# Order of the products in the first MLP unit: the product without inner weights is put first and held until its group is done

## The chip, the cores and the metric

The kernel runs on one core of a Trainium2 chip. The metric is the device time of that core in microseconds (us), from a run of the whole program. The engines are named as in the profile: PE is TensorE's matmul, PEld its weight load, DVE is VectorE, ACT is ScalarE, POOL is GpSimd, SP is SyncE (here an issuer of DMAs only).

## The reference, cut to what matters

There are two layers on x of shape (2, 512, 32, 32). Layer 0 is a deformable attention with a position bias from a small network, followed by an MLP; layer 1 is a single-head self-attention over 1024 positions. The change is in the MLP of layer 0:

```
x = x + out                                   # after the attention of layer 0
xn2 = _bn(x, bn2_g, bn2_b)
h1 = gelu(einsum('bchw,oc->bohw', xn2, mlp_w1) + mlp_b1)      # 512 -> 2048 channels
return x + einsum('bchw,oc->bohw', h1, mlp_w2) + mlp_b2       # 2048 -> 512
```

## The kernel before, in words

The MLP is cut into eight units: `units` holds (b, p) for two images b and four slices p of 512 hidden channels (L970). The loop over the units (L1185) loads the weights of later units, calls `layer1` for the slice's first matrix product with its gelu, and `layer2` for the second. Both are 512x512 by 512x1024 products in float32, done by Strassen's scheme in the form with seven block products: `PARTS` (L112) gives for product 1 to 7 the weight block and the data block, each an input quarter or a sum of quarters (`fold`, `spread`).

`layer1` applies the scheme twice. Six of the seven products (1 and 6, 4 and 7, 5 and 3, three groups) are themselves cut into seven small products by `twice` (L141). The weight blocks of these six need sums of their own quarters, the "inner weights" `we` (tile `w1e`): `load_inner` (L986) copies three quarters by DMA from SP and adds others on top by four accumulating DMAs from POOL (`gather`, L973), one after the other. The data blocks' inner sums are in `xe`, computed on DVE by `part` (L1082). The seventh product, number 2, is a plain one of 8 matmul instructions in the trace (L1073), with the weight quarter `w[:, 0]` and the data block `xb[:, 0]`, which are no sums. In the kernel before it is `second` (L1124): product into PSUM, added by DVE onto `c11`, then gelu of block 0.

The order is written out by hand. `STEPS` (L139) gives each of a group's seven small products a place in time: steps 1, 2, 6, 5, 7, 4, 3 at 0, 1, 3, 4, 6, 9, 12; group g is put 7g later, so that three groups interleave, and `fills` are put among them by the number that they carry: `second` at 21, and for the first unit of each image the parts 1 and 2 of the data sums at 4 and 10. Each entry's matmuls are chained behind the newest TensorE instruction, so TensorE keeps this order strictly. The other engines' order is chosen by the language's scheduler. In order of time (P2 is `second`):

```
place      0  1  2  3  4  5  6  7  8  9 10 11 12 13 14 15 16 17 18 19 20 21 22 23 24 25 26
group 0    1  2     6  5     7        4        3
group 1                         1  2     6  5     7        4        3
group 2                                              1  2     6  5     7        4        3
fill                                                                     P2
```

Within a group, steps 1, 6, 7 and 4 add up in one PSUM bank and are copied out by ACT in between (L166, L170, L172, L176), each before the next may add; steps 2, 5 and 3 are taken up by DVE (`plus`, L137). The last of them calls `done(g)` (L1110), which puts the groups' results together in `hm`:

- group 0 writes `c11` and `c12` (hm 0 and 1), group 1 `c21` and `c22` (hm 2 and 3), group 2 `r5` and `r3` (hm 4 and 5);
- `done(0)` adds c11 to c12; `done(1)` makes c22 and c21 and gives gelu of block 2; `done(2)` makes c22 and c12 and gives gelu of blocks 3 and 1.

`spread` then makes hm 4, 5, 3 and 6 out of the blocks, and `layer2` (L1133) multiplies them with `w2t` in the order of products 2, 1, 3, 5, 6, 7, 4, which read hm 2, 0, 3, 4, 5, 1, 6.

PSUM tiles of two banks come in turn from four buffers (`Turns`, L46 and L1184): `twice` takes two for each group, `second` one, `layer2` seven, 14 a unit. Before the first unit, TensorE does `project` (L1014), the output projection of the attention, whose last matmuls are at L1020.

Of the kernel before, what the change touches and what calls it, by code (L numbers as in the profile page):

```python
# [8 lines left out]
F32 = mybir.dt.float32  # L9
# [5 lines left out]
P = 128  # L15
# [42 lines left out]
def conv_seq_kernel(ctx: ExitStack, tc: tile.TileContext, x, xt, kst, pst, cst, vec, wsm, outw, w1, w2, wl, wlt, brow, out):  # L58
    nc = tc.nc
# [4 lines left out]
    def newest(engine):  # L64
        return next(i for i in reversed(nc.cur_bb.bb.instructions) if i.engine == engine)
# [8 lines left out]
    def col(name, i=0):  # L74
        return vs[:, VOFF[name] + i : VOFF[name] + i + 1]
# [60 lines left out]
    def plus(out, a, b_, op=ALU.add):  # L136
        nc.vector.tensor_tensor(out, a, b_, op)  # L137
# [3 lines left out]
    def twice(pool, sets, weights, moving, dest, done, fills=(), sign=-1.0):  # L141
        todo = [(7 * g + t, g, q) for g in range(len(sets)) for t, q in STEPS]
        todo += [(t, None, fill) for t, fill in fills]
        held = {}
        for _, g, q in sorted(todo, key=lambda e: e[0]):
            with tc.issue_after(newest(mybir.EngineType.PE)):
                if g is None:
                    q()
                    continue
                if q == 1:  # L150
                    held[g] = pool.tile([P, 2, 512], F32, tag="ps2", name="sw")
                if q == 2:
                    held[g, 2] = pool.tile([P, 2, 512], F32, tag="ps2", name="sw")
                bank = {2: lambda: held[g, 2][:, 0], 5: lambda: held[g, 2][:, 1], 3: lambda: held[g, 2][:, 1]}.get(
                    q, lambda: held[g][:, 0]
                )().rearrange("p (e n) -> p e n", e=2)
                s, t = PARTS[q]
                for e, p in enumerate(sets[g]):
                    for k, (w, x) in enumerate(zip(weights(p, s), moving(p, t))):
                        nc.tensor.matmul(  # L160
                            bank[:, e, :], w, x, start=(q in (1, 2, 5) and e == k == 0), stop=True,
                            skip_group_check=True,
                        )
            d11, d12, d21, d22 = (dest(g, m, h) for m in range(2) for h in range(2))
            if q == 1:
                nc.scalar.copy(d11, bank)  # L166
            elif q == 2:
                plus(d11, d11, bank)
            elif q == 6:
                nc.scalar.copy(d12, bank)  # L170
            elif q == 7:
                nc.scalar.activation(d22, bank, AF.Copy, scale=sign)  # L172
                b5 = held[g, 2][:, 1].rearrange("p (e n) -> p e n", e=2)
                plus(d22, d22, b5, ALU.subtract if sign < 0 else ALU.add)
            elif q == 4:
                nc.scalar.activation(d21, bank, AF.Copy, scale=sign)  # L176
            elif q == 3:
                plus(d12, d12, bank)
                done(g)
# [27 lines left out]
    with tc.tile_pool(name="lp", bufs=2) as lp:  # L207
# [381 lines left out]
        def weights(i):  # L589
            ps = [flat("psg") for _ in range(2)]  # L590
            for o in range(NCH):
                for k in range(NCH):
                    if i == 0 and (o, k) in ((1, 0), (3, 1)):
                        yield
                    nc.tensor.matmul(  # L595
                        ps[k // 2][:, k % 2 * 512 : k % 2 * 512 + 512], wls[i][:, 0, o, k * P : (k + 1) * P],
                        wls[i][:, 1, o, :], start=(o == 0), stop=(o == NCH - 1),
                    )
            yield
            for k2 in range(2):  # L600
                nc.scalar.copy(gs[:, i, 2 * k2 : 2 * k2 + 2, :].rearrange("p k o -> p (k o)"), ps[k2])
            yield
            nc.gpsimd.dma_start(out=gdr[i], in_=gs[:, i])
# [282 lines left out]
        for s in range(NS):  # L886
# [29 lines left out]
            if bg is None and s > ready and (s - ready) % 4 == 0 and (s - ready) // 4 <= 8:  # L916
                i = (s - ready) // 4 - 1
# [50 lines left out]
    with ExitStack() as top, tc.tile_pool(name="wp", bufs=1) as wp:  # L968
# [100 lines left out]
        def product(w, x):  # L1069
            def go(ps, a, b_):  # L1070
                for m in range(2):
                    for k in range(2):
                        nc.tensor.matmul(  # L1073
                            ps[:, m, :], w[:, a, k, m * P : (m + 1) * P], x[:, b_, k, :],
                            start=(k == 0), stop=(k == 1),
                        )
            return go
# [8 lines left out]
            part(0)  # L1086
            return xe, part

        def layer1(p, we, w, xb, xe, hm, others=()):
            def gelu(blk, src, scale=1.0):  # L1090
                for m in range(2):
                    nc.scalar.activation(
                        hm[:, blk, m, :], src[:, m, :], AF.Gelu,
                        bias=col("mb1", 4 * p + 2 * (blk // 2) + m), scale=scale,
                    )

            c11, c12, c21, c22, r5, r3 = (hm[:, j] for j in range(6))

            def weights(q, j):
                a = FIRST_W[PARTS[q][0]]  # L1100
                return [inner_w(w, we, a, a - 1)[j]]

            def moving(q, j):
                b_ = FIRST_X[PARTS[q][1]]
                return [inner_x(xb, xe, b_, b_ - 1)[j]]

            def dest(g, m, h):
                return hm[:, 2 * g : 2 * g + 2, m, 256 * h : 256 * h + 256]

            def done(g):  # L1110
                if g == 0:
                    plus(c12, c12, c11)
                elif g == 1:
                    plus(c22, c22, c12)
                    plus(c21, c21, c22)
                    gelu(2, c21, -1.0)
                else:
                    plus(c22, c22, r5)
                    gelu(3, c22, -1.0)
                    plus(c12, c12, r5)  # L1120
                    plus(c12, c12, r3)
                    gelu(1, c12)

            def second():  # L1124
                ps = mq.tile([P, 2, 512], F32, tag="ps2", name="sw")
                product(w, xb)(ps, 0, 0)
                plus(c11, c11, ps)
                gelu(0, c11)

            twice(mq, ((1, 6), (4, 7), (5, 3)), weights, moving, dest, done, ((21, second), *others))  # L1130
            spread([hm[:, j] for j in range(7)])

        def layer2(b, p, w, hm):  # L1133
# [41 lines left out]
        xb = normalise(0)  # L1175
        spread(op1[1])
        project(1, *op1, op1w[:, 3:5].rearrange("p a k n -> p a (k n)"))
        xe, part = sums(xb)
# [5 lines left out]
        mq = Turns([ctx.enter_context(tc.tile_pool(name="mq", bufs=1, space=PSUM)), zp, zp, zp])  # L1184
        for i, (b, p) in enumerate(units):  # L1185

            j, k = divmod(i, NCH)
            if k == 0:
                br = cp.tile([P, C], F32, tag="kz", name="br")
                nc.sync.dma_start(out=br, in_=brow[j].partition_broadcast(P))  # L1190
            wr = f_pool.tile([P, C], F32, tag="ss", name="wr")
            nc.sync.dma_start(out=wr, in_=wlt[:, i])
            with tc.issue_after(copied[-1]) if i else nullcontext():
                load_first(i + 1)
            wa, we, wb = wts.pop((b, p))
            hm = cp.tile([P, 7, 2, 512], F32, tag="big", name="hm")
            layer1(p, we, wa, xb, xe, hm, ((4, lambda: part(1)), (10, lambda: part(2))) if p == 0 else ())
            if i == NU:
                with tc.issue_after(newest(mybir.EngineType.DVE)):
                    finish(0)  # L1200
            load_inner(i + 1)

            with tc.issue_after(newest(mybir.EngineType.DVE)):
                nc.vector.scalar_tensor_tensor(
                    wr, wr, 1.0, br, ALU.mult, ALU.mult, accum_out=ub[:, j, k : k + 1]
                )
            if p == NU - 1 and b == 0:
                xb = normalise(1)
            layer2(b, p, wb, hm)
            load_second(i + 1)  # L1210
            if i == NU:
                with tc.issue_after(newest(mybir.EngineType.SP)):
                    gg = f_pool.tile([P, 7, 2, 256], F32, tag="vp", name="gg")
                    load_g(gg, 0)
            if i == NU + 2:
                xbl = blocks(0)
            if p == NU - 1 and b == 0:
                xe, part = sums(xb)
# [6 lines left out]
    with tc.tile_pool(name="sp", bufs=1) as sp:  # L1225
        for b in range(B):
# [180 lines left out]
            def moving(p, j):  # L1407
                g, e = where[p]
                x = ax(g, PARTS[p][1])[j] if j < 4 else (x45[g][:, 0], x45[g][:, 1], inner["x"][g])[j - 4][:, e]
                return [x[:, k] for k in range(2)]  # L1410
# [173 lines left out]
```

## Time and profile before

| | |
|---|---|
| median of 3 runs (lowest to highest) | 2621.48 us (2620.96 to 2621.51) |
| the profiled execution's own time | 2623.41 us |
| its span, first to last instruction | 2621.6 us |
| PE busy in the span | 2597.2 us, 99% |
| PEld, DVE, ACT, POOL busy | 1004.4, 2311.3, 1745.7, 981.8 us |
| mean granted TensorE clock | 0.999 |
| matmuls of `twice` in the first unit | from 1944.60 us of the span on |
| first matmul of `layer2` in the first unit | 1970.74 us |

The profile is one execution of the program. A busy PE is not PE at its peak, since matmuls are pipelined; so the idle time of PE and the granted clock in a stretch are read from the timeline and the windows rather than from the share. A row of a timeline has the start in us from the span's start, the length, the engine, the line in the kernel, the operation, what is written and read, shapes, the count of instructions merged into the row, and in brackets the idle time before it with what ended it. One logical float32 matmul appears as two matmul instructions.

### The profile page before, as it was taken

To read this page: it belongs to the slowest core of one execution; us is meant where nothing else is said; L and a number is where in the kernel's file an instruction comes from. 1 tells how busy PE (TensorE), PEld (TensorE's weight loads), DVE (VectorE), ACT (ScalarE), POOL (GpSimd) and SP (SyncE) were. 2 spreads that over 40 slices of the span, in tenths; PEclk is the share of its full clock that TensorE was granted. 3 is DMA by queue.
4 is the path that set the end of the run, shared out by engine and by line. 5 is a ranking of instruction groups with operands and counts; after the bars stand their busy time and mean duration, and the time that the engine had idled before them with its cause. 6 is when DMAs were issued, how large, how long until landed. Compare 5 with 4: busy or idle time off the path is not lost.

```text
span 2621.6 us, 48901 instructions
## 1 busy us (share of the span) xinstructions
PE 2597.2 (99%) x19648; PEld 1004.4 (38%) x19648; DVE 2311.3 (88%) x1462; ACT 1745.7 (67%) x2324; POOL 981.8 (37%) x1121
## 2 busy tenths in 40 slices
PE   9999999999999999999999999999999999999999
PEld 3332322233233233322233332332355665646556
DVE  7999999999999999999999999898776587666656
ACT  5887898888887888888887777777723242314041
POOL 1344544444445444444444454333332334200100
PEclk9999999999999999999999999999999999999999
DMA  5888988999999999899898999787777768400202
GB/s 190 174 191 186 213 183 184 195 200 201 189 191 194 188 204 195 180 190 201 186 202 181 196 193 193 163 181 166 160 198 162 153 139 177 90 16 0 73 0 57
DMA packets 177522, 428.27 MB, mean 163 GB/s; under 512 B 29936, under 2 KB 78208, under 8 KB 174608
## 3 DMA queue, kind: packets, MB, share of 16 engines
q0 software_dynamic: 107392, 273.09, 58.2%
q1 hardware_dynamic: 69472, 151.75, 17.4%
q8 instruction: 155, 2.54, 0.4%
q14 instruction: 71, 0.58, 0.1%
q10 hardware_dynamic: 432, 0.31, 0.0%
HBM read 82.16 MB, written 6.55 MB: 34 GB/s over the span
## 4 chain that ended last, share of the span: by engine, by line
PE 63%; DVE 12%; issue 10%; DMA 9%; POOL 4%; ACT 2%; DVEq 0%; SPq 0%; POOLq 0%; ACTq 0%
PE ps L693 37%; PE sw L1073 7%; PE sw L1234 7%; PE sw L160 6%; DVE h L676 5%; DMA u<-uc 3%; DVE ub L713 2%; POOL u L732 2%; PE sw L1332 2%; DMA u<-u 1%; PE psg L595 1%; DMA uc<-uc 1%; DVE hm L137 1%; DVE uo L713 1%; DMA w1e<-w1e 1%
## 5 line engine op out<-in xcount | busy, mean ns | idle before, releaser
L693 PE MATMUL ps<-h,cw 128*32 128x512 f32 x16384 | 1775.2, 593 | 10.8 <-ACT rx L703 7.7
L676 DVE CUSTOM_DVE_ANT_1 h<-ta,tb 128x4096 f32<-128x4096 f32 (+1 forms) x257 | 1130.1, 4398 | 20.8 <-PE ps L693 16.8
L693 PEld LDWEIGHTS ps<-h,cw 128*32 128x32 f32 x16384 | 525.7, 110 | 1229.3 <-issue 1132.9
L703 ACT ACTIVATE rx<-ps,sc 128x1024 f32<-128x1024 f32 x512 | 567.6, 1109 | 155.9 <-PE ps L693 97.5
L732 POOL DMA_DIRECT2D u<-u x397 | 410.1, 1516 | 14.6 <-DMA u<-ub 12.1
L705 ACT ACTIVATE ub<-ps,sc 128x1024 f32<-128x1024 f32 x256 | 307.8, 1202 | 84.0 <-PE ps L693 82.6
L713 DVE SCALAR_TENSOR_TENSOR ub<-rx,sc,ub 128x1024 f32<-128x1024 f32 x256 | 326.2, 1274 | 10.5 <-ACT ub L705 10.5
L715 POOL DMA_DIRECT2D uo<-ub x127 | 112.1, 883 | 584.2 <-DVE ub L713 536.7
L1073 PE MATMUL sw<-hm,w2t 128*128 128x512 f32 x448 | 193.9, 592 | 0.4 <-DVE hm L125 0.2
L705 ACT ACTIVATE uo<-ps,sc 128x1024 f32<-128x1024 f32 x128 | 153.9, 1202 | 42.4 <-PE ps L693 39.7
L713 DVE SCALAR_TENSOR_TENSOR uo<-rx,sc,uo 128x1024 f32<-128x1024 f32 x128 | 163.2, 1275 | 5.0 <-ACT uo L705 5.0
L732 POOL DMA_DIRECT2D u<-uc x126 | 126.8, 1269 | 19.4 <-DMA u<-uc 17.9
L715 POOL DMA_DIRECT2D uc<-ub x64 | 56.1, 877 | 199.7 <-DVE ub L713 158.9
L1073 PEld LDWEIGHTS sw<-hm,w2t 128*128 128x128 f32 x448 | 85.0, 190 | 104.8 <-issue 98.7
L137 DVE TENSOR_TENSOR hm<-hm,sw 128x512 f32<-128x512 f32 (+1 forms) x80 | 58.6, 737 | 74.4 <-PE sw L160 54.7
L715 POOL DMA_DIRECT2D u<-ub x64 | 55.4, 866 | 168.5 <-DVE ub L713 164.8
L732 POOL DMA_DIRECT2D uc<-uo x63 | 103.1, 1637 | 16.8 <-DMA uc<-uo 16.5
L732 POOL DMA_DIRECT2D uc<-uc x63 | 104.5, 1659 | 2.0 <-DMA uc<-ub 2.0
L1398 POOL DMA_DIRECT2D xs<-rs x6 | 7.2, 1200 | 258.1 <-DVE rs L137 258.1
L705 ACT ACTIVATE uc<-ps,sc 128x1024 f32<-128x1024 f32 x64 | 76.9, 1202 | 26.4 <-PE ps L693 16.6
L656 ACT ACTIVATE ta<-fb,vs 128x512 f32<-128x512 f32 (+1 forms) x65 | 89.2, 1376 | 6.5 <-DMA fb<-fdr 6.5
L732 POOL DMA_DIRECT2D u<-uo x63 | 83.3, 1322 | 24.7 <-DMA u<-uo 19.2
(294 smaller groups left out, 2624.9 us busy)
## 6 DMA issues: line engine op xcount, KB each, us to landing
uo<-ub POOLq DMA_DIRECT2D x127, 512.0 KB, 5.3
fb<-fdr SPq DMA_DIRECT2D x64, 512.0 KB, 6.1
u<-ub POOLq DMA_DIRECT2D x64, 512.0 KB, 6.7
uc<-ub POOLq DMA_DIRECT2D x64, 512.0 KB, 6.0
u<-u POOLq DMA_DIRECT2D x63, 256.0 KB, 7.0
u<-uo SPq DMA_DIRECT2D x63, 256.0 KB, 5.8
u<-uo POOLq DMA_DIRECT2D x63, 256.0 KB, 7.3
uc<-uc POOLq DMA_DIRECT2D x63, 256.0 KB, 8.0
```

Source lines behind the costliest of these rows:

```text
L137: nc.vector.tensor_tensor(out, a, b_, op)
L160: nc.tensor.matmul(bank[:, e, :], w, x, start=(q in (1, 2, 5) and e == k == 0), stop=True, skip_group_check=True,)
L656: nc.scalar.activation(ta.rearrange("p j x -> p x j")[:, :, j0:j1], fb[:, 0, :, j0:j1], AF.Identity, bias=col("cb1"), scale=col("w1x"),)
L676: nc.vector._custom_dve(TENSOR_ADD_SAT, out=h1[:, y : y + step].rearrange("p y t x -> p (y t x)"), in0=a.unsqueeze(1).to_broadcast([P, ste ...
L693: nc.tensor.matmul(ps[32 * q : 32 * q + 32, h, :], cw2[:, 32 * z : 32 * z + 32], h1[:, 16 * h : 16 * h + 16, q, :], start=True, stop=True,)
L703: nc.scalar.activation(o, ps, AF.Relu, bias=sc[:, 4 + z : 5 + z])
L705: nc.scalar.activation(o, ps, AF.Relu, bias=sc[:, 4 + z : 5 + z], scale=sc[:, z : z + 1])
L713: nc.vector.scalar_tensor_tensor(r[1], r[0], sc[:, z : z + 1], r[1], ALU.mult, ALU.add)
L715: nc.gpsimd.dma_start(out=sums[s][1], in_=sums[s][3], accum_op=ALU.add)
L732: nc.gpsimd.dma_start(out=out, in_=in_, accum_op=ALU.add)
L1073: nc.tensor.matmul(ps[:, m, :], w[:, a, k, m * P : (m + 1) * P], x[:, b_, k, :], start=(k == 0), stop=(k == 1),)
L1234: nc.tensor.matmul(ps[:, m, :], w[:, a, k, c + m * P : c + (m + 1) * P], x[b_][:, k, :], start=(k == 0), stop=(k == nk - 1),)
```

## The change

For the first unit alone (`i == 0`), product 2 is no longer done late, at 21, but before everything else, at -1. Its result can't be added to `c11` then, since group 0 has not written it. It is copied by ACT from PSUM to `r3` (hm 5), which group 2 will write later, and added to `c11` by DVE at 13.5: after `done(0)`, which must read c11 without it, and before the first step of group 2, whose copy overwrites part of `r3`. The gelu of block 0 follows there. In the other seven units nothing is changed.

```diff
-        def layer1(p, we, w, xb, xe, hm, others=()):
+        def layer1(p, we, w, xb, xe, hm, others=(), early=False):
...
-            twice(mq, ((1, 6), (4, 7), (5, 3)), weights, moving, dest, done, ((21, second), *others))
+            def first():
+                ps = mq.tile([P, 2, 512], F32, tag="ps2", name="sw")
+                product(w, xb)(ps, 0, 0)
+                nc.scalar.copy(r3, ps)
+
+            def merge():
+                plus(c11, c11, r3)
+                gelu(0, c11)
+
+            plain = ((-1, first), (13.5, merge)) if early else ((21, second),)
+            twice(mq, ((1, 6), (4, 7), (5, 3)), weights, moving, dest, done, (*plain, *others))
...
-            layer1(p, we, wa, xb, xe, hm, ((4, lambda: part(1)), (10, lambda: part(2))) if p == 0 else ())
+            layer1(p, we, wa, xb, xe, hm, ((4, lambda: part(1)), (10, lambda: part(2))) if p == 0 else (), i == 0)
```

## The prediction, made before the result was known

> **What bounds the kernel now.** I read the chain of work that ended last in order of time, then TensorE's own timeline around the start of the MLP, then the windows with the granted clock, then the timelines of VectorE and ScalarE. Columns of the chain and the timelines: start, length, what; in brackets the idle time before and its releaser.
>
> ```profile
> 1936.84 5.60 DMA w1e<-w1e
> 1942.72 13.25 DMA w1e<-w1e
> 1956.02 9.72 PE sw L160 x36
> 1965.74 3.43 PE sw L1073 x8
> 1970.90 24.03 PE sw L1073 x56
> ```
>
> The last sum of the inner weights of unit 0 is issued at 1942.72 and lands 13.25 us later. From 1956.02 on the chain is TensorE nearly without a break to the end of the kernel, so a microsecond saved or lost in unit 0 of the MLP is one of the total. TensorE in unit 0:
>
> ```profile
> 1944.60 1.89 PE L160 MATMUL sw<-xb,w1x 128*128 128x256 f32 x8
> ...
> 1956.02 1.13 PE L160 MATMUL sw<-xb,w1e 128*128 128x256 f32 x4 [2.19 <-DMA w1e<-w1e]
> 1956.98 4.44 PE L160 MATMUL sw<-xb,w1x 128*128 128x256 f32 x12
> 1961.26 1.03 PE L160 MATMUL sw<-xe,w1x 128*128 128x256 f32 x4
> ...
> 1963.85 1.03 PE L160 MATMUL sw<-xb,w1e 128*128 128x256 f32 x4
> ...
> 1965.58 3.60 PE L1073 MATMUL sw<-xb,w1x 128*128 128x512 f32 x8
> ...
> 1970.74 24.20 PE L1073 MATMUL sw<-hm,w2t 128*128 128x512 f32 x56
> ```
>
> Layer 1 lasts from 1944.60 to 1970.74, 26.14 us. Its work: one step of `twice` is 4 records in 0.86 us (1961.26 to 1962.12), 21 steps 18.1; the whole product at L1073 3.44 (1965.58 to 1969.01 for 8 records); together 21.56. So 4.58 us are lost: 2.19 in the wait for the weights, 1.69 in the 12 matmuls behind it (4.44 where the same group takes 2.75 elsewhere), 0.41 at the second pair of steps, 0.29 in crumbs. The 1.69 is the clock; its column is the one before the DMA share:
>
> ```profile
> 1957.00:1958.00 1.00, 1.00 (x5) 0.85 (x4) 0.71 (x2) 0.00 (x0) 0.63 (x1) 0.70 0.78 131
> 1958.00:1959.00 1.00, 1.00 (x4) 0.81 (x3) 1.00 (x1) 0.48 (x1) 0.00 (x0) 0.50 0.99 166
> 1960.00:1961.00 1.00, 1.00 (x4) 0.82 (x3) 0.00 (x0) 0.58 (x1) 0.33 (x1) 0.59 0.36 59
> ```
>
> Half speed from about 1957.4 to 1960.8, just after the gap. What VectorE and ScalarE do there decides the rest:
>
> ```profile
> 1957.19 0.69 DVE L137 TENSOR_TENSOR hm<-hm,sw 128x512 f32<-128x512 f32 x1 [5.15 <-PE sw L160]
> 1957.98 1.23 DVE L137 TENSOR_TENSOR hm<-hm 128x1024 f32<-128x1024 f32 x1
> 1959.15 0.69 DVE L137 TENSOR_TENSOR hm<-hm,sw 128x512 f32<-128x512 f32 x1
> ...
> 1965.78 0.60 ACT L172 ACTIVATE hm<-sw 128x512 f32<-128x512 f32 x1 [2.00 <-PE sw L160]
> 1966.39 1.28 ACT L1092 ACT_TABLE_LOAD   x1
> 1968.70 1.33 ACT L1092 ACTIVATE hm<-hm,vs 128x512 f32<-128x512 f32 x2 [1.02 <-DVE hm L137]
> ```
>
> The three VectorE rows are step 3 of group 0 taken up, done(0), and step 7 of group 1; on ScalarE the first gelu brings a table load, which runs when the instruction before it is over.
>
> **What the skill says.** The Trainium skill, "TensorE: Matmul & The Clock Gate", section "Part 1: The HAM clock gate", has two clock states, half after an idle window of about 3.4 us and full after a busy one. The trace agrees in the two states (1.00 and 0.50) and in the length of the low stretch (3.4 us), but here a gap of 2.19 us was enough. "ScalarE: Activation LUTs", section "What ACT_TABLE_LOAD costs", gives about 1.28 us for the load and as much again for a drain; the trace shows 1.28 and no drain beside it, so I use 1.28. "PSUM — Partial Sum Buffer", section "Engine vs sequencer instructions", calls the queues of ScalarE and VectorE strictly first in, first out; the timelines show no exception, and so a copy behind a gelu waits for the gelu.
>
> **The change part by part.**
>
> *The product moved to the front.* 8 matmul records, 3.44 us, at 1944.60: its weight quarter and its block of xb are there (w1x was loaded before its first sum at 1909.94, xb normalised by 1926.5), so nothing holds it. No DMA, SP or POOL instruction moves with it; the weights land at 1956.0 as before. Step 1 of group 0 starts at 1948.04. On ScalarE the new copy into r3 (128x1024, 1.01 us by the rows of L1138) ends about 1949.25, the copy of step 1 thus at 1949.8, and step 6 starts 0.15 late. VectorE's sums for xe now end before the take-up of step 2, so the 0.41 goes. Ten steps (8.63) then bring step 3 of group 0 to t = 1956.8. That is 0.8 after the landing: **the 2.19 goes, and its 1.69 with it**. If the landing came 0.8 later, part of it would be back.
>
> *The merge between the groups.* r3 lies where step 1 of group 2 is copied to (hm 4 and 5). So that copy waits for the merge on VectorE, and TensorE's step 6 of group 2, which adds on the same bank, waits for the copy. Without a wait it would come five steps after t, at t + 4.31. By the rows above: step 3 is taken up at t + 1.17, done(0) starts at t + 1.96, step 7 of group 1 at t + 3.13, the merge about t + 3.73, and ends at t + 4.96. Then ScalarE: the gelu pair of block 0 comes ahead of the copy in the program and is ready at the same moment, 1.33; the copy 0.58. The trace doesn't show this order. From both sides: copy first, TensorE goes on at t + 5.6 (stall 1.3); gelu first with its table load done while ScalarE was idle, t + 6.96 (2.65); gelu first with the copy of step 4 of group 1 (L176) ahead of both, t + 8.4 (4.1), for then the load starts only after L176: ready at t + 4.5, done t + 5.1, load to 6.4, gelu to 7.75, copy to 8.3. I take the last, because L176 is ready 0.45 before the merge ends and ScalarE is then idle. Behind the waiting step on TensorE is everything else. **+4.1.**
>
> *The clock after that gap.* 4.1 us is longer than the 2.19 that halved it before. The low stretch 1957.4 to 1960.8 gives windows that end at 1964.2 and 1967.6; the gap lies from 1961.1 to 1965.2, so half speed holds from 1964.2 to 1967.6, of which 2.4 us carry work. **+1.2** (between 0, no drop, and 1.7 as before).
>
> *The tail of layer 1.* The whole product stood between steps 7 and 4 of group 2 and covered two waits. Let s be the start of step 3 of group 1 (1963.85 before). The gelu of block 2 began at s + 4.85 (1968.70), its first half ends at s + 5.6, and layer 2's first product reads that. Before, layer 2 came at s + 6.89, so it was hidden by 1.3. Now four steps follow s, 3.45 us, and layer 2 can't start before s + 5.6: **+2.15**. The wait of step 4 for ScalarE's copy of step 7 (0.9) lies inside this. Later products of layer 2 need block 3 (about s + 8.2) and the spread (from s + 11.7) at s + 12.5 and later: no stall.
>
> *Downstream.* As many PSUM tiles per unit as before, the inner weights are freed at the same distance from layer 2: I cost it at nothing. The cover is the waiting time of the landed weights: unit 1's last sum is issued at 1990.84, and needed at 2003.66.
>
> *Sum.* Lost after: 0.15 + 4.1 + 1.2 + 2.15 = 7.6, before 4.58: **+3.0 us**. Layer 2 starts at about 1973.75 instead of 1970.74. The profiled execution took 2623.41 us (span 2621.6 and 1.8 around it) and would become 2626.4; the median of the runs is 2621.48 and becomes 2624.5, +0.11%. A measurement of this kernel tells some 0.2% from no change, 5.2 us; this is under it.
>
> **Rivals.**
> *A, table load hidden* (gelu ahead of L176): the stall is 2.65, and the clock drops for 1.7 or not at all: 0.15 + 2.65 + 1.7 + 2.15 = 6.65, +2.1, or +0.4. 2621.9 to 2623.6. For it: the load before ran without waiting. Against: L176 is ready earlier.
> *B, copy ahead of the gelu*: the stall is 1.3, too short for a clock drop: 0.15 + 1.3 + 2.15 = 3.6, -1.0. 2620.5. Against: later in program order.
> *C, the waits don't bind*: only 0.15 is lost, -4.4, 2617.1. It needs the copy of step 1 without the merge and block 2 a full 2 us earlier; the VectorE rows speak against both.
> *D, the clock makes it slower beyond doubt.* The profiled execution was 1.93 us longer than the median, about the clock's 1.69. If the timed runs don't have that drop, there is 1.69 less to win: +4.7, 2626.2; and if the tail's idle time of 2.15 halves the clock once more, +1.7: 2627.9, slower by 0.25%. It decides from gaps of about 2.2 us inside one window. Against: the runs agree within 0.6 us, so the drop comes in all or none, and the tail's gap is broken by two steps.
>
> **How the numbers follow.** Forecast 2624.5: 0.42. A 0.22, B 0.16, C 0.07, D 0.13. The range from 2620.3 to 2626.6 holds the forecast, A, B and the lower half of D, and leaves out C and the rest of D, some 0.14. Faster by over 0.2% (under 2616.2) asks for more than all that is lost: 0.02. Slower (over 2626.7) is the upper half of D: 0.07. Within: 0.91.
>
> **What would show it.** In the profile after: first product at about 1944.6; no wait for w1e at the third step of group 0; a gap of 4 us (A 2.65, B 1.3) before step 6 of group 2, released by ScalarE; the table load after L176; a low clock after it; layer 2 starting 5.6 us after step 3 of group 1, released by the gelu; its start at 1973.75. Wrong would be: the weights landing later than 1956.8, the gap absent, or new waits from unit 1 on.

## The result, and the profile after

| | before | after |
|---|---|---|
| median of 22 runs each (lowest to highest) | 2621.41 us (2620.12 to 2623.74) | 2625.38 us (2623.22 to 2626.82) |
| the profiled execution's own time | 2623.41 us | 2626.42 us |
| its span | 2621.6 us | 2624.7 us |
| first unit: first matmul of layer 1 to that of unit 1 | 1944.60 to 1994.77, 50.17 us | 1945.51 to 1998.26, 52.75 us |

The ratio of the times is 1.0015, with a 95% interval from 1.0009 to 1.0021: 4.0 us more, where 3.0 was predicted. The two spans differ by 3.1 us: 0.91 before the first unit begins, 2.58 in it, and -0.39 behind it. The change shows in the first unit alone.

TensorE's timeline after (columns as before):

```profile
1945.51 3.60 PE L1073 MATMUL sw<-xb,w1x 128*128 128x512 f32 x8
...
1957.84 1.03 PE L160 MATMUL sw<-xb,w1e 128*128 128x256 f32 x4
...
1961.30 1.03 PE L160 MATMUL sw<-xe,w1x 128*128 128x256 f32 x4
1966.12 3.78 PE L160 MATMUL sw<-xe,w1e 128*128 128x256 f32 x8 [3.80 <-ACT hm L166]
1969.70 1.91 PE L160 MATMUL sw<-xb,w1e 128*128 128x256 f32 x4
1971.40 1.11 PE L160 MATMUL sw<-xb,w1x 128*128 128x256 f32 x4
1972.39 1.13 PE L1073 MATMUL sw<-hm,w2t 128*128 128x512 f32 x2
1973.35 1.03 PE L160 MATMUL sw<-xe,w1x 128*128 128x256 f32 x4
```

The whole product comes first. The step that waited 2.19 us for the inner weights in the kernel before (here at 1957.84) waits for nothing. In its place step 6 of group 2, due at 1961.30 + 0.86 = 1962.16, starts at 1966.12, released by ScalarE's copy. The rows behind it are slow: 8 records in 3.58 us where they take 1.73 elsewhere. And the records at L1073 that read `hm` are layer 2: they stand among the last steps of layer 1.

The chain of waits (start, length, what) goes from TensorE to ScalarE and back (L176 a copy, the piece without a tile the table load, the pair the gelus of block 0, L166 the copy that TensorE waits for):

```profile
1962.36 0.60 ACT hm L176
...
1962.97 1.28 ACT L1092
...
1964.27 1.33 ACT hm L1092 x2
1965.60 0.48 ACT hm L166
...
1966.12 6.39 PE sw L160 x16
```

VectorE's timeline in the same stretch, done(0) and the merge:

```profile
1959.70 1.23 DVE L137 TENSOR_TENSOR hm<-hm 128x1024 f32<-128x1024 f32 x1
...
1961.44 1.22 DVE L137 TENSOR_TENSOR hm<-hm 128x1024 f32<-128x1024 f32 x1
```

The last VectorE row is the merge, over at 1962.66. From the due time to it 0.50; until L176 is over 0.30; the table load 1.29; the gelu pair 1.26; the copy 0.56 (its row in the timeline is 1965.51 to 1966.07); TensorE's start 0.05: 3.96 us. The windows (busy share and count of PE, PEld, DVE, ACT, POOL, then the granted clock, DMA share, GB/s):

```profile
1964.00:1965.00 1.00, 0.00 (x0) 0.00 (x0) 0.00 (x0) 0.99 (x3) 0.00 (x0) 0.87 0.76 131
...
1968.00:1969.00 1.00, 1.00 (x4) 0.82 (x3) 0.00 (x0) 0.59 (x1) 0.00 (x0) 0.50 0.00 0
...
1971.00:1972.00 1.00, 1.00 (x5) 0.86 (x4) 0.35 (x1) 0.00 (x0) 0.00 (x0) 0.72 0.00 0
```

A clock of 0.87 is half speed for the last 0.26 us of its slice, 0.72 half speed for the first 0.56: low from about 1964.74 to 1971.56, 6.8 us, twice the 3.4 of the kernel before. The 16 records of layer 1 between 1966.12 and 1972.39 took 6.27 us where four steps take 3.45, so the low clock costs about 2.8 us in this execution.

**The account.** The unit's work is 21.56 (layer 1) + 24.08 (layer 2, 56 records of 0.43) = 45.64 us. Lost before: 50.17 - 45.64 = 4.53. Lost after: 52.75 - 45.64 = 7.11, of which 3.96 gap, 2.8 clock, and 0.28 behind the first copy (60 records of `twice` in 13.22 us, 12.94 of them work). For the end of layer 1 next to nothing is left, about 0.1.

### The profile page after: what moved, and what is told of

It reads as the page before. It is cut to its first block, busy times and chain, and to the rows that moved or that the text cites. A ratio compares the mean times of both kernels' runs of the same rounds, so it can differ in the third digit from the quotient of the medians.

```text
span 2624.7 us, 48900 instructions
## 1 busy us (share of the span) xinstructions
PE 2597.7 (99%) x19648; PEld 1005.3 (38%) x19648; DVE 2308.9 (88%) x1462; ACT 1748.3 (67%) x2325; POOL 977.8 (37%) x1121
## 4 chain that ended last, share of the span: by engine, by line
PE 75%; DVE 10%; issue 7%; DMA 4%; POOL 2%; ACT 2%; DVEq 0%; ACTq 0%; POOLq 0%; SPq 0%
PE ps L693 47%; PE sw L1073 7%; PE sw L160 7%; PE sw L1244 7%; DVE h L676 4%; PE sw L1020 2%; PE sw L1342 2%; DVE ub L713 2%; DMA u<-uc 1%; POOL u L732 1%; PE psg L595 1%; DMA u<-u 1%; PE sim L823 1%; DVE uo L713 1%; DVE hm L137 1%
## 5 line engine op out<-in xcount | busy, mean ns | idle before, releaser
L1073 PE MATMUL sw<-hm,w2t 128*128 128x512 f32 x448 | 194.3, 593 | 0.2 <-DVE hm L125 0.2
L137 DVE TENSOR_TENSOR hm<-hm,sw 128x512 f32<-128x512 f32 x79 | 57.6, 732 | 79.0 <-PE sw L160 54.4
L1073 PEld LDWEIGHTS sw<-hm,w2t 128*128 128x128 f32 x448 | 84.9, 190 | 103.9 <-issue 97.3
(295 smaller groups left out, 2621.9 us busy)
```

What stands on the lines that cost most here:

```text
L1073: nc.tensor.matmul(ps[:, m, :], w[:, a, k, m * P : (m + 1) * P], x[:, b_, k, :], start=(k == 0), stop=(k == 1),)
```

## The experiments

**The theory**: the gap comes from holding product 2 in `r3`, which the copy of step 1 of group 2 overwrites, so that merge, table load and gelu pair all stand ahead of TensorE's step 6; the clock falls because of the gap. **Rivals:** the place of the product itself costs (it stands ahead of the steps, and no longer covers the end); or the low clock comes from the change of order, not from the gap. Beside these, one question of the baseline: is the low clock of the kernel before in its timed runs, or in its profiled execution alone? Below, "the unit" is the length of the first unit in the profiled execution, and an interval is 95%, of the ratio to the kernel before as it ran beside the experiment (medians 2621.33 beside 1 to 4, 2621.30 beside 5 to 8, 2622.11 beside 9 and 10).

**1. Held in a bank that nobody writes.** `hm[:, 6]` is free until the end of the unit, so the copy of group 2 has no merge to wait for.

```
-                nc.scalar.copy(r3, ps)
+                nc.scalar.copy(hm[:, 6], ps)
-                plus(c11, c11, r3)
+                plus(c11, c11, hm[:, 6])
```

> Product 2 is held in hm 6, which nothing writes before the spread, in place of r3; all else as in the change. Theory (the loss is the copy of group 2's step 1 queued behind merge, table load and gelu, and the low clock after that gap): no gap before step 6 of group 2, no low clock, first unit (first matmul of layer 1 to first matmul of unit 1) 46.2 to 47.8 us against 52.91 with the change and 50.17 before; time about 2617.5 to 2619. Rival (what costs is that product 2 no longer stands in the tail of layer 1, and the extra copy): 2624 or more.

Measured: 2620.47 us, ratio 0.9997 (0.9989 to 1.0005); the unit took 47.41 us, 5.34 less than with `r3` (the 52.91 of the expectation ran to the end of the unit's last matmul; to the first matmul of unit 1, as for all others, it is 52.75). The time is above the 2617.5 to 2619 expected, since that was reckoned from a baseline which experiment 5 corrects. TensorE:

```profile
1961.45 2.28 PE L160 MATMUL sw<-xe,w1e 128*128 128x256 f32 x8
...
1965.42 1.10 PE L1073 MATMUL sw<-hm,w2t 128*128 128x512 f32 x2 [0.83 <-ACT hm L170]
```

Step 6 of group 2 comes when it is due, the clock stays full, and what is left is 0.38 in the row of 2.28 (1.89 elsewhere) and 0.83 ahead of the first records of layer 2. 3.96 + 2.8 went, and some 1.4 came. The gap and the low clock belong to `r3`. The place of the product costs in this unit no more than it gains by covering the wait for the weights (47.41 us against 47.77 and 48.56 in experiments 5 and 6); in units without that wait it does cost, as experiment 10 shows.

**2. Held in `r3`, gelu left where it was.** The merge stays at 13.5, the gelu of block 0 goes back to 21, behind the copy.

```
-                gelu(0, c11)
-            plain = ((-1, first), (13.5, merge)) if early else ((21, second),)
+            plain = ((-1, first), (13.5, merge), (21, lambda: gelu(0, c11))) if early else ((21, second),)
```

> Product 2 still held in r3 and merged at 13.5, but the gelu of block 0 is placed at 21, so the copy needn't wait for table load and gelu. Theory: the gap shrinks from 4.0 to about 1.3 us (merge and copy alone), too short for a low clock; first unit about 47.5 us, time about 2619. Rival (the wait for the merge is what counts, gelu and table load are beside it): gap about 4, time about 2625.

Measured: 2620.61 us, ratio 0.9995 (0.9987 to 1.0003); the unit 47.48 us.

```profile
1962.84 1.99 PE L160 MATMUL sw<-xe,w1e 128*128 128x256 f32 x8 [1.16 <-ACT hm L166]
```

The wait for the merge alone leaves a gap of 1.33 against the due time 1961.51, and no low clock: the gap and the time of rival B (1.3, 2620.5). The time is above the 2619 expected, for the same reason as in 1. Of the 3.96 us some 2.6 are thus the load and the gelu pair ahead of the copy.

**3. The table loaded ahead of time.** A gelu of one element in `first`, written where nothing reads it, brings the load into idle time; the gelu pair stays ahead of the copy.

```
                 nc.scalar.copy(r3, ps)
+                nc.scalar.activation(uc[:, 0:1], xb[:, 0, 1, 511:512], AF.Gelu)
```

> The change plus a one-element gelu on ScalarE while it is idle before layer 1, so that the table load is done there. Theory: gap 2.7 us in place of 4.0, released by the same copy; the clock still drops, for one window or two; first unit 50.3 to 51.6 us, time 2622.5 to 2624. Rival (ScalarE is not the one waited for): no change, 2625.4.

Measured: 2622.89 us, ratio 1.0005 (0.9997 to 1.0013); the unit 50.37 us. Its TensorE row, then its window with the low clock:

```profile
1964.78 3.46 PE L160 MATMUL sw<-xe,w1e 128*128 128x256 f32 x8 [2.38 <-ACT hm L166]
```

```profile
1965.00:1966.00 1.00, 1.00 (x4) 0.80 (x4) 0.45 (x1) 0.00 (x0) 0.00 (x0) 0.57 1.11 193
```

The gap is 2.55, so the load was worth 1.4. The clock still falls, at about 1965 (0.57), for one stretch of 3.4 us and not two. This is rival A (2.65 and 1.7; 2623.6) in size.

**4. The gap filled.** Eight matmul records that nothing needs stand at 16.5, with their own PSUM tile; nothing else is changed.

```
+            def busy():
+                ps = mq.tile([P, 2, 512], F32, tag="ps2", name="sw")
+                product(w, xb)(ps, 0, 0)
+
-            plain = ((-1, first), (13.5, merge)) if early else ((21, second),)
+            plain = ((-1, first), (13.5, merge), (16.5, busy)) if early else ((21, second),)
```

> The change plus eight unneeded matmul records (3.4 us) put in the gap before step 6 of group 2; their result is not used. Theory: the useful work waits as long as before (4.0 us) but TensorE stays busy, the clock stays full, and 2.8 us are saved: first unit about 50.1 us, time about 2622.6. If the clock costs only the 1.2 us of the prediction: about 2624.2. If it costs nothing: 2625.4.

Measured: 2623.86 us, ratio 1.0009 (1.0001 to 1.0017); the unit 50.34 us.

```profile
1961.85 3.70 PE L1073 MATMUL sw<-xb,w1x 128*128 128x512 f32 x8 [0.69 <-ACT hm L176]
1965.39 1.89 PE L160 MATMUL sw<-xe,w1e 128*128 128x256 f32 x8
```

Step 6 now comes 4.39 us after it is due (1961.00), later than in the changed kernel, and yet the unit is 2.41 us shorter: the records behind it run at full clock (1.89, not 3.78). The low clock follows from TensorE's idle time, not from the order, and costs in the two profiles what the account says (2.41 + 0.43 more wait = 2.84). In the medians the difference is only 2625.38 - 2623.86 = 1.52, which makes 1.95 for the clock: less than the expected 2.8, and the first sign that not every timed run of the changed kernel has the 6.8 us.

**5. The kernel before once more**, with only a comment changed.

```
-# ---- launch: one core ----
+# ---- launch: one core, again ----
```

> The kernel before once more, for more executions and their clocks. If the low clock after the 2.19 us gap comes in every execution, the profiled one has the first unit at 50.2 us again and lies near the median. If it depends on how the gap falls, an execution without it has the first unit at about 48.5 us, and the median run is nearer to that; then the change costs about 1.7 us more in the median than in the two profiles.

Measured: 2621.49 us, ratio 1.0000 (0.9992 to 1.0008). But its profiled execution took 2621.22 us, not 2623.41, and the unit 47.77, not 50.17:

```profile
1956.38 1.13 PE L160 MATMUL sw<-xb,w1e 128*128 128x256 f32 x4 [1.47 <-DMA w1e<-w1e]
1957.34 2.75 PE L160 MATMUL sw<-xb,w1x 128*128 128x256 f32 x12
```

The work ahead ended 1.07 us later in this execution (the unit starts at 1945.67), the wait for the weights is 1.47 and not 2.19, and the 12 records behind it take 2.75 and not 4.44. One program, two profiled executions, 2.2 us apart.

The timed runs say which is the rule, by their mean granted clocks, which are on record to three places. A stretch of 3.4 us at half speed takes 1.7 us of 2621, or 0.00065, from the mean; a run shown as 1.000 has lost less than 1.3 us in all, so it had no such stretch. Of the 95 timed runs of this kernel in experiments 1 to 8 (41 and 41 beside them, 13 here) 54 are shown as 1.000. The other 41, at 0.999, may have had one or not, since the clock is also low at the very end of the kernel, which takes 0.35 to 1.62 us in the profiles of before, after and 1 to 8.

**6. The wait of the kernel before filled** with four unneeded records at 11.5 in a spare PSUM bank (`spare` keeps the open banks; `fill` is `((11.5, busy),)` in the first unit and empty in the others).

```
+            def busy():
+                for k in range(2):
+                    nc.tensor.matmul(spare[-1][1][:, 1], w[:, 0, k, 0:P], xb[:, 0, k, :], start=(k == 0), stop=(k == 1))
...
-            twice(mq, ((1, 6), (4, 7), (5, 3)), weights, moving, dest, done, ((21, second), *others))
+            twice(mq, ((1, 6), (4, 7), (5, 3)), weights, moving, dest, done, ((21, second), *fill, *others))
```

> The kernel before with four unneeded matmul records (1.7 us) put in the gap before the third step of group 0; their result is not used. Theory (the clock falls after the gap): wait for the weights as before, clock full, first unit 48.3 to 48.6 us. In the median 1.7 us less than before if the low clock came in every run of it, about the same if it came in few.

Measured: 2621.50 us, ratio 1.0003 (0.9995 to 1.0011); the unit 48.56 us. Its lines are numbered two higher:

```profile
1956.64 1.13 PE L162 MATMUL sw<-xb,w1e 128*128 128x256 f32 x4 [0.47 <-DMA w1e<-w1e]
```

There is no gap that could lower the clock, and the median is that of the kernel before. Had its timed runs carried the 1.69, taking it away would have shown as about that much.

**7. Experiments 1 and 3 together**: `hm[:, 6]` and the table loaded early, which are the two diffs above.

> Product 2 held in hm 6 and the gelu table loaded while ScalarE is idle before layer 1. Theory: of the 1.8 us that were still lost with hm 6 alone (0.8 before a matmul of layer 2 behind step 7's copy chain, 0.4 at step 5), about 1.2 go: first unit 46.3 us, time about 2619.3, faster than both kernels. Rival (ScalarE's queue has no part in it): 47.4, 2620.5.

Measured: 2619.57 us, ratio 0.9994 (0.9986 to 1.0002); the unit 46.43 us, 0.8 above its work. It is the shortest of all and 5.8 us below the changed kernel; from the kernel before the interval doesn't tell it apart.

**8. The same with layer 2 behind layer 1.** In the changed kernel the scheduler put four records of layer 2 among the last steps. Here, on top of 7, the matmuls of layer 2 in the first unit are chained behind the newest TensorE instruction.

```
-            layer2(b, p, wb, hm)
+            with tc.issue_after(newest(mybir.EngineType.PE)) if i == 0 else nullcontext():
+                layer2(b, p, wb, hm)
```

> The same with all matmuls of layer 2 in the first unit chained behind layer 1's last. If the four records of layer 2 that the scheduler puts between steps 7, 4 and 3 are what covers the tail of layer 1: 0.9 to 2.2 us longer than without the chain, first unit 47.2 to 48.5. If the tail needs no cover: the same.

Measured: 2620.87 us, ratio 0.9997 (0.9989 to 1.0006); the unit 47.49 us, 1.06 more than in 7.

```profile
1966.64 1.13 PE L160 MATMUL sw<-xe,w1x 128*128 128x256 f32 x4 [0.69 <-ACT hm L172]
...
1968.77 24.20 PE L1073 MATMUL sw<-hm,w2t 128*128 128x512 f32 x56
```

```profile
1968.91 1.33 ACT L1092 ACTIVATE hm<-hm,vs 128x512 f32<-128x512 f32 x2 [0.51 <-DVE hm L137]
```

Step 4 waits 0.69 for ScalarE, where in 7 two records of layer 2 stand. So the mixing hides a wait at the end of layer 1; here, with the table loaded early, 1.06 us of it. The second view is the gelu of block 2: layer 2 has begun before it, without a wait, so its first records can't be those that read block 2.

**9. The change in all eight units** (`i == 0` becomes `True`), to see the gap eight times.

```
-            layer1(..., i == 0)
+            layer1(..., True)
```

> The change in all eight units. In units 1 to 7 there is no wait for weights to win and no table load. Theory (copy behind merge and gelu, then the clock): each has a gap of about 2.6 us before step 6 of group 2 and, where the gap fills enough of a clock window, a low clock for 1 to 2 us: each 2.7 to 4.5 us longer than its 46.3, together 19 to 31, time 2644 to 2657. Rival (the loss of the change is an accident of the first unit): within 5 us of 2625.

Measured: 2667.02 us, ratio 1.0174 (1.0159 to 1.0189): 44.9 us more, over the 2644 to 2657 expected. Four rows of TensorE's timeline, in units 1, 2, 7 and 8, then one of VectorE's adds in the second unit:

```profile
1965.64 3.39 PE L160 MATMUL sw<-xe,w1e 128*128 128x256 f32 x8 [3.80 <-ACT hm L166]
...
2016.94 3.78 PE L160 MATMUL sw<-xe,w1e 128*128 128x256 f32 x8 [3.61 <-ACT hm L166]
...
2283.30 1.99 PE L160 MATMUL sw<-xe,w1e 128*128 128x256 f32 x8 [2.38 <-ACT hm L166]
...
2333.87 3.59 PE L160 MATMUL sw<-xe,w1e 128*128 128x256 f32 x8 [2.38 <-ACT hm L166]
```

```profile
2010.71 2.13 DVE L137 TENSOR_TENSOR hm<-hm 128x1024 f32<-128x1024 f32 x1
```

The gap is there in every unit, 2.38 to 3.80 us, 25.8 in sum by the waits. I had taken shorter gaps for the later units; in the second one GpSimd adds weight sums of layer 2 from 2010.17 to 2017.41, and beside it done(0) and the merge, the two adds ahead of the gelu pair, take 2.13 and 1.69 in place of 1.23. The low clock comes on top where it comes: of two gaps of the same 2.38 us one is followed by it (3.59) and one is not (1.99).

The first unit is that of the changed kernel, with the same gap of 3.80, and yet its clock is low for one stretch of 3.4 us alone, from 1965.08 to 1968.5. The 16 records behind the gap take 5.03 us and not 6.27, and the unit 51.51 and not 52.75. What differs is where the gap lies: here 0.56 us of it fall inside the low stretch, in the profile of the changed kernel 1.38. The other units agree, read in windows of 0.02 us. The clock was low for 6.8 us in units 2, 4 and 5, where 0.66, 0.67 and 0.91 us of the gap fall inside, and for 3.4 us in units 3, 6 and 8, where it is 0.21, nothing and 0.15 (unit 7 has no low stretch).

**10. Experiment 1 in all eight units.**

> Product 2 first and held in hm 6 in all eight units. No gap by the theory; what is left is the tail that product 2 no longer covers: 0.2 us in a unit in which records of layer 2 are put into it, up to 2.2 in one without. Time 2622 to 2632 where the first unit alone gave 2620.5. If the tail needs no cover: 2620.5.

Measured: 2638.17 us, ratio 1.0066 (1.0049 to 1.0082), 16.1 us more; over the 2622 to 2632 expected. TensorE in the second unit:

```profile
2010.76 1.13 PE L160 MATMUL sw<-xe,w1e 128*128 128x256 f32 x4 [1.64 <-DVE hm L137]
2011.72 1.03 PE L160 MATMUL sw<-xb,w1e 128*128 128x256 f32 x4
...
2017.35 7.99 PE L1073 MATMUL sw<-hm,w2t 128*128 128x512 f32 x18 [0.76 <-ACT hm L1092]
```

Two things cost here. The merge stands ahead of a take-up in VectorE's queue and is slowed beside GpSimd (1.64 of wait; I had not counted it). And in this unit no record of layer 2 stands among the last steps: layer 2 starts 5.63 us after step 3 of group 1 (2011.72), released by the gelu. So where there is no wait for weights to cover, the early place of the product is a loss, some 2.4 us in each of the seven units added (16.1 us above the kernel before, where experiment 1 was 0.9 below it).

## Why the prediction was right, and where its steps were not

The total was right, 2624.5 against 2625.38 in a range to 2626.6, and so was the mechanism of its largest term, the gap. That the total came this near is in part luck. Two terms were wrong by about 2 us each, in opposite directions, and nearly cancel: between the two profiles +3.0 was put and 2.58 measured. The third error, in the base, is the main reason why the median rose by 4.0 us and not by the 2.6 of the profiles.

- **The product moved to the front: right.** The wait for the weights is gone; the product's copy costs 0.28 where 0.15 was put. The margin was 0.8 us in the prediction; in the profile the last sum was issued at 1943.07 and landed 12.7 us later, about 1955.8, and the third step of group 0 came at 1957.84, so it was 2 us.
- **The gap of 4.1: right**, 3.96, in the order taken: L176, load, gelu pair, copy. Its parts were shown one by one: a free bank takes all of it (1), the copy ahead of the gelu leaves 1.33 (2), the load hidden leaves 2.55 (3). The choice between the three orders, which rested on L176 being ready before the merge ends, held: L176 started 0.30 before the end.
- **"The clock after that gap", +1.2: too small by 1.6 in the profile.** The drop came, but lasted 6.8 us. The prediction took one low stretch of 3.4 us on the grid of the execution before, with 1 us of it still in the gap. The stretch began 2.4 us after TensorE went idle; that it is followed by a second one fits the 1.4 us of idle time that reach into it, since in experiment 3, where none does, there was one stretch only. The units of experiment 9 bear this out: one stretch with up to 0.56 us of idle time in it, two with 0.66 or more. No run set that time on purpose. The upper bound of 1.7 was wrong for the same reason: it counted one stretch. In the timed runs the clock costs less, about 2 us by the medians of the changed kernel and experiment 4.
- **"The tail of layer 1", +2.15: too large by about 2.** The gelu of block 2 came when it was put, at s + 4.84 in experiment 8 (s + 4.85), and where layer 2 begins with that block it starts at s + 5.63 (experiment 10; s + 5.6). The wrong step was that layer 2 begins with it: in experiment 8 it starts at s + 4.70, before that gelu. TensorE's order is written by hand only inside `twice`. Layer 2's matmuls have no such chain, and the scheduler put those that needed only product 1 and block 0 between steps 7, 4 and 3 of group 2. The gelu of block 0 comes early in the changed kernel, so they had their data. Experiment 8 takes the mixing away and pays 1.06 us of the tail. What the step missed is that the change, by finishing block 0 early, also made work that fills the tail.
- **The base, 1.69 of 4.58.** The sum was made against a profiled execution with a low clock that more than half of the timed runs don't have. Experiments 5 and 6 show it from two sides, and the mean clocks of the runs from a third; and median less unit is 2572.5 to 2573.7 us in the changed kernel and experiments 1 to 8, but 2571.2 with the unit of the first profile of before. With 2573.0 for all, an estimate, the unit takes 48.4 us in the median run of the kernel before, near the 47.77 and 48.56 of experiments 5 and 6, and 52.4 in that of the changed kernel. The first half of rival D was thus true, for which the agreement of the runs within 0.6 us had been taken as evidence against. It is none: three runs may agree by chance (22 spread over 3.6 us), and agreeing with each other they need not be like the profile.
- **Chances.** Rivals A and B were real orders, and the sizes of their gaps were right: experiments 3 and 2 have them, at 2622.89 (2621.9 to 2623.6 put) and 2620.61 (2620.5 put). That these totals fit is luck again, since both hold the 2.15 of the tail and rest on the base of 4.58, each nearly 2 us too large. Rival C, 2617.1, was not reached even in 7: that is 1.8 us below the kernel before by the medians, not 4.4.
- **Downstream: right.** From the second unit on no new wait appears; the last part of the span is 0.39 shorter, no more than two executions differ by.

Not every timed run of the changed kernel has both low stretches. One of the 22, the fastest at 2623.22, is shown with a mean clock of 1.000, so it had none; four, at 2625.45 to 2626.50, are shown as 0.998, a loss of about 3.9 us or more, which is more than one stretch (1.7) and the end of the kernel (at most 1.62 in the profiles) take together. The first unit of experiment 9 had one. The other 17 runs, at 0.999, can't be told apart, so how often each case comes stays open.

## What to carry to other kernels

A result that is parked in a tile which someone writes later ties that writer to everything queued ahead of the release: list every instruction on each queue between the last read and the writer, the table load of an activation among them, and park it in a tile that nobody needs instead. Before costing a low clock, look whether it is in the timed runs: a profiled execution that is longer than the median by about its price is the sign, and the mean clock of each run can say it. And where only a part of an engine's order is pinned, work of the next stage may fill a hole that you have costed; look which of it is ready.

## What the runs showed of the hardware

- The granted clock fell after gaps of TensorE of 2.19, 2.38 and 3.80 us, and did not after 1.16, 1.47, 1.64 and another of 2.38. The Trainium skill, "TensorE: Matmul & The Clock Gate", section "Part 1: The HAM clock gate", asks for an idle window of about 3.4 us; the low stretches here do last 3.4 or 6.8 us, but a gap clearly shorter than a window was enough, and the same gap falls on both sides. What separates the cases in these traces is where the gap lies. In experiment 9 the low stretches begin at 1965.08, 2016.28, 2070.90, 2122.10, 2176.70, 2231.32 and 2333.72, which are 51.2, 54.6 or 102.4 us apart, 15, 16 or 30 times 3.413. In the 3.41 us ahead of each first low stretch, these and those of the other three profiles, TensorE was idle for about 2.0 us or more; the gap of 2.38 without one falls on that grid as 1.6 and 0.8.
- VectorE's add of 128x1024 took 1.23 us alone and 1.64 to 2.67 beside GpSimd's adds (experiments 9 and 10). The skill, "SBUF — State Buffer", section "SBUF: two separate sides", has the two engines share a port pair that one holds for a whole instruction, against VectorE's operations with two SBUF inputs too; the trace agrees in the direction, and the delay on an add was at most 1.44 us. VectorE's adds of 128x512 with one input in PSUM were not slower beside them (0.67 to 0.69 us).
- The table load of 1.28 us can be moved: a gelu of one element placed earlier brings it into idle time (at 1928.43 in experiment 3), and the true gelu then follows the copy ahead of it without a load. Where it is not moved, the gelu pair starts 0.02 us after the load's end (1964.25 to 1964.27 in the changed kernel): no drain shows between them.
